# Batch 0's projection by seven block products, its value blocks copied by GpSimd in the setup

## The chip, the core and the metric

The kernel runs on one core of a Trainium2 chip. The core has five engines with a queue of instructions each: TensorE (PE; its weight loads are listed as PEld), VectorE (DVE), ScalarE (ACT), GpSimd (POOL) and SyncE (SP), which here only issues DMAs. An instruction starts when its predecessor on the same engine has been issued and the semaphores that it waits for are set. The metric is the device time of one execution in microseconds, the median of three runs.

## The reference

A graph attention layer over 16 batches of 512 nodes with 512 features. `cond` is one vector for each batch, `mask` an integer tensor of 512 x 512 x 11.

```python
self_feat = concat(x, where(x.sum(-1) == 0, 0, cond)) @ W_self.T + b_self   # (16, 512, 512)
output = self_feat
for d in range(2):                       # adjacency and its transpose
    A = adj[:, :, :20]                   # only the first 20 nodes are keys
    q = self_feat @ Wq[d].T + bq[d]      # 16 heads of 32
    k = self_feat[:, :20] @ Wk[d].T + bk[d]
    aff = where(A.sum(-1) > 0, q.k / sqrt(32), -9e15) + (A @ w_bias + b_bias)
    w = softmax(aff)                     # over 20 keys
    out = (w @ self_feat[:, :20]) through Wout[d], head by head, + bout[d]
    output += out
return x + relu(output)
```

## The kernel before

All data are float32 and features lie on the partitions (`P` = 128, `C` = 4 chunks of features). Queries are never formed: in the **setup** the keys are multiplied through `Wq` into a matrix for each batch (`g`, 128 x 4 x 608), and the values through `Wout` (`vw_d`, in HBM). A batch then needs `self_feat` (tile `sf`), the scores `sf` x `g`, a softmax, and a product with the values.

**Setup** (lines 458 to 764). After the first projections a loop of 22 *bursts* (`keys`, L674) makes the key matrices, three halves at a time: 12 matmuls into two PSUM tiles, which ScalarE (L689) and VectorE (L691) empty into staging tiles `st` (four buffers). From the staging tiles the key matrix goes to three places: for batch 0 into the SBUF tile `g0` (by SP DMAs for three of four feature chunks, by a GpSimd copy for the last), for batch 1 into `g1_d` and for the rest into `g_d`, both in HBM. All bursts use the same two PSUM tiles, so a burst starts when the previous one is emptied.

Between bursts TensorE does other work, which the string `plan` (L719) spreads over the bursts from the fifth on, one word for each burst: `v` and `w` are value steps (L649; a `w` is half of the rows), `c` score-bias steps (L622), `n` row flags (L189), `s` a quarter of one piece of batch 0's projection, `b` small biases on VectorE. GpSimd stores values and score biases in HBM by its own DMAs (L657, L636).

**Projection.** `self_feat` of the batches 1 to 15 is made by a scheme with seven block products in place of eight (`product`, L249): the weights and the columns of x after the first 20 are cut in 2 x 2 blocks, GpSimd forms sums of the x blocks (`x_sum`, L238, t1 to t4) and of the weight blocks (`weight_sums`, L223, once), TensorE does seven products of 16 matmuls of 246 columns (in the order 1, 2, 6, 7, 5, 4, 3), and VectorE puts the PSUM results together (`partial`, L289, which reads the bank that later products keep adding to, and `joined`, L299, which adds the other bank). A product that adds to a bank waits until the partial before it has read it. Batch 0 uses the plain projection instead (`self_feat`, L205, 128 matmuls of 236 or 256 columns): three quarters in the setup, the last at tile 1 of batch 0 in the loop. The first 20 columns are a copy of the setup's key features (`new_self`, L303).

**Loop** (lines 786 to 984). Each batch has four tiles (`nt`) of 128 nodes. A tile is: scores on TensorE (L365, two PSUM buffers of two banks), mask and bias added on VectorE (L379, with `full`, formed by GpSimd at L344), maximum and subtraction (L383, L387), exponential on ScalarE (L392), sum and reciprocal on VectorE (L415, L416), normalising on GpSimd (L417), transposing on VectorE (L424). The product with the values of batch b - 1 (`attend`, L435) stands at tile 2 of batch b, and the projection of batch b + 1 is spread over the tiles 2 and 3 of batch b and tile 0 of b + 1.

**Values.** `attend` wants the values in blocks with zeros between them. `clear_blocks` writes zeros over all of `bd_d` in HBM (2 MB), `blocks` copies the values of all batches from `vw_d` into it, HBM to HBM, in runs of 128 bytes by 12 DMAs, and `load_values` brings the blocks of one batch in.

**Queues.** The order on each queue is written out by hand. In the later batches a load on SP waits for a named instruction (`behind`), so that loads come one by one: for instance the first half of the next batch's mask after `done["masks"]`. In batch 0 SP instead issues, unthrottled: all keys of batch 1 ahead of the loop, at tile 1 the masks, score biases, the 2 MB of zeros and the row-sum inputs (`load_xn`), at tile 2 the 12 block copies, at tile 3 the values of batch 0. `row_sum` (L169, ScalarE) reads what `load_xn` brings; `mask_spread` (L337, ScalarE) copies the summed mask to the layout that `full` needs.

Of the kernel before, what the change touches and what calls it, by code (L numbers as in the profile page):

```python
# [13 lines left out]
P = 128  # L14
# [4 lines left out]
def gat_kernel(  # L19
# [64 lines left out]
    vw_d = dram.tile([2, C, BM, P], F32, name="vw_d")  # L84
    bd_d = dram.tile([C, B, 32, HL, 2, DH], F32, name="bd_d")
# [5 lines left out]
    adds, fulls, wts, outs, held, sf_ps, conds, prods = {}, {}, {}, [], [None] * 3, {}, {}, {}  # L91
    sums, parts, us, done = {}, {}, {}, {}
# [42 lines left out]
    def load_values(b, ins=None):  # L135

        vds[b] = gp.tile([P, HL, 2, DH], F32, tag="vd", name=f"vd{b}", bufs=1)
        for c in range(C):
            behind(nc.sync.dma_start(
                vds[b][bass.ts(c, 32)].rearrange("p e i g -> p (e i g)"), bd_d[c, b].rearrange("r e i g -> r (e i g)")  # L140
            ), ins if c == 0 else None)

    def clear_blocks(zero):

        nc.sync.dma_start(
            bd_d.rearrange("c b r e i g -> (c b r) (e i g)").rearrange("(n p) w -> p n w", p=P),
            zero.unsqueeze(1).to_broadcast([P, C * B * 32 // P, HL * 2 * DH]),
        )

    def blocks():  # L150

        bb = bd_d.rearrange("c b r e i g -> (c b) r e i g")
        vv = vw_d.rearrange("d c (b m) (e g) -> d (c b) m e g", m=NG, e=HL)
        for e in range(HL):
            for i in range(2):
                j = (e * S) // 32 + i
                for d in range(2):
                    lo = max(e * S + d * NG, 32 * j)
                    hi = min(e * S + (d + 1) * NG, 32 * j + 32)
                    if lo < hi:  # L160
                        m, r = lo - e * S - d * NG, lo - 32 * j
                        nc.sync.dma_start(bb[:, r : r + hi - lo, e, i], vv[d, :, m : m + hi - lo, e])


# [29 lines left out]
    def self_feat(b, f, h, parts=((0, range(C)), (1, range(C)))):  # L194


        lo, hi = max(NG, h * N // 2), (h + 1) * N // 2
        for i, ks in parts:
            if (i, ks[0]) == (0, 0):
                if (f, h) == (0, 0):  # L200
                    new_self(b)
                held[0] = bank(f"ps_sf{b}_{f}{h}", 3 if (f, h) == (1, 1) else None)
            for k in ks:
                for a in range(HL):
                    nc.tensor.matmul(  # L205
                        held[0][bass.ts(a, R), i * N // 2 : i * N // 2 + hi - lo],
                        ws_v[:, k, bass.ds((2 * f + i) * P + a * R, R)], xs[b][:, k, lo:hi],
                        start=(k == 0), stop=(k == C - 1),
                    )
            if (i, ks[-1]) == (1, C - 1):  # L210
                sf_ps[b, f, h] = held[0]

    def self_copy(b, f, h):

        lo, hi = max(NG, h * N // 2), (h + 1) * N // 2
        ps = sf_ps.pop((b, f, h))
        for i in range(2):
            nc.vector.scalar_tensor_tensor(
                sfs[b][:, 2 * f + i, lo:hi], nzs[b][:, lo:hi], qw[:, 2 * f + i, b : b + 1],
                ps[:, i * N // 2 : i * N // 2 + hi - lo], ALU.mult, ALU.add,  # L220
            )

# [15 lines left out]
    def x_sum(b, n):  # L238

        t = sums[b, n] = xsum.tile([P, 2, HN], F32, tag=f"t{n}", name=f"t{b}_{n}")  # L240
# [8 lines left out]
    def product(b, n):  # L249
# [11 lines left out]
        if n == 1:  # L261
            parts[b, "a"] = [bank(f"ps_a{b}_{i}", i) for i in range(2)]
        if n == 2:
            parts[b, "d"] = bank(f"ps_d{b}", 2)
        if n == 5:
            parts[b, "c"] = bank(f"ps_c{b}", 3)
# [30 lines left out]
    def joined(b, n, key, f, l):  # L297

        done["joined"] = nc.vector.tensor_add(  # L299
            block(b, f, l), parts[b, key][:, : 2 * HN].rearrange("p (i n) -> p i n", i=2), us.pop((b, n))  # L300
# [30 lines left out]
    def mask_spread(b, h, quarters=range(4)):  # L331

        add = conds[b, h]
        for a in quarters:
            for g in range(HL):
                r = bass.ts(g, R)
                nc.scalar.copy(adds[b, h][bass.ts(a, R), :, g], add[r].rearrange("p (t m) -> p t m", t=2))  # L337
# [38 lines left out]
    def weigh(b, nt, ps, between=None):  # L376

        f = softmax_view(fulls.pop((b, nt)))
        nc.vector.tensor_add(  # L379
# [78 lines left out]
    with tc.tile_pool(name="setup", bufs=1) as sp, tc.tile_pool(name="ps_acc", bufs=4, space=PSUM) as acc["pool"]:  # L458
# [157 lines left out]
        with tc.tile_pool(name="setup_g", bufs=4) as sg:  # L616

            def bias_scores(d):
# [7 lines left out]
                if d == 0:  # L626
                    stages["c"] = load.tile([P, 2, F], F32, tag="xn", name="c")
                    nc.gpsimd.memset(stages["c"][:, :, :BM], 0.0)
# [12 lines left out]
            def values(t, ds, k):  # L641
# [11 lines left out]
                if k == C - 1:  # L653
                    v = msk.tile([P, H * S], F32, tag="full", name=f"v{t}{ds[0]}")[:, :F]
                    nc.vector.tensor_copy(v, ps)
                    for i, d in enumerate(ds):
                        nc.gpsimd.dma_start(  # L657
                            vw_d[d, :, bass.ds(t * P, rows)].rearrange("c r w -> r c w"),
                            v[bass.ds(i * rows, rows)].rearrange("p (c w) -> p c w", c=C),
                        )  # L660

            stages = {}
            HB = B // 2

            def keys(runs):
# [14 lines left out]
                for fc, hg, d, lo, hi in runs:  # L680
# [12 lines left out]
                    if d == 1 and hi == 2:  # L693
                        to, of = g0[:, fc, bass.ts(hg, WD // C)], st[:, 0].rearrange("p h d m -> p (h d m)")
                        if fc < C - 1:
                            nc.sync.dma_start(to, of)
                        else:
                            nc.gpsimd.tensor_copy(to, of)
# [3 lines left out]
            def self_step(b, f, h, i, k):  # L702
                self_feat(b, f, h, ((i, (k,)),))
                if (i, k) == (1, C - 1):
                    self_copy(b, f, h)
# [6 lines left out]
                "s": [  # L712
                    (self_step, (0, f, h, i, k)) for f, h in ((0, 0), (1, 0), (0, 1))
# [353 lines left out]
```

## Time and profile before

| | |
|---|---|
| runs (us) | 585.79, 588.49, 589.13; median 588.49 |
| profiled execution (us) | 586.05 |
| its span, first to last instruction (us) | 583.9 |
| busiest engines | TensorE 575.7, VectorE 489.0, ScalarE 395.6, GpSimd 384.9 |
| HBM read, written | 82.30 MB, 40.24 MB |
| batch period from batch 1 on (us) | 30.5 |

How to read it: times are microseconds from the start of the span. TensorE executes a float32 matmul as two records, so 16 matmuls of a block product appear as x32. The four matmuls of a group work on different columns of the array at the same time, so the length of a piece in the chain, not the mean of one record, is what the piece costs. SPq and POOLq are the DMA-issuing sides of those queues; a DMA has an issue time on its queue and a time to landing.

### The profile page before, as it was taken

The numbers are of one execution on the slowest core, as the hardware profiler recorded it, in microseconds if no ns is written. First come the engines' busy times: TensorE is split into PE (matmuls) and PEld (weight loads), VectorE is DVE, ScalarE is ACT, GpSimd is POOL, SyncE is SP. The second block draws the span as 40 slices with busy tenths as digits, with TensorE's granted clock in tenths as the row PEclk, the third lists the DMA queues.
The fourth block names the chain that finished last, engine by engine and source line by source line (L and its number), as shares of the span: only waits on it lengthen the run. The fifth ranks groups of instructions, "written<-read, shape, count | busy, mean of one in ns | idle before, by whom it ended". The sixth has DMA issues, their size and how long they took to land.

```text
span 583.9 us, 30310 instructions
## 1 busy us (share of the span) xinstructions
PE 575.7 (99%) x13184; PEld 437.0 (75%) x13184; DVE 489.0 (84%) x783; ACT 395.6 (68%) x1162; POOL 384.9 (66%) x351
## 2 busy tenths in 40 slices
PE   9999999999999999999999999999999999999996
PEld 6654547887878787877878787787887878787873
DVE  0485565889898989899999999898989898989895
ACT  1334644586877777868686868687786877777671
POOL 2405663648778685858586777686868677776775
PEclk9999999999999999999999999999999999999999
DMA  8999899857766675757576767676676765664404
GB/s 303 388 407 311 331 377 320 273 123 213 209 197 196 185 214 169 217 167 217 168 214 171 214 171 212 177 199 188 199 202 187 199 198 172 199 199 114 144 15 146
DMA packets 103220, 124.14 MB, mean 213 GB/s; under 512 B 21712, under 2 KB 71920, under 8 KB 101040
## 3 DMA queue, kind: packets, MB, share of 16 engines
q1 hardware_dynamic: 101296, 119.79, 66.8%
q8 instruction: 104, 1.70, 1.3%
q0 software_dynamic: 672, 1.36, 1.0%
q10 hardware_dynamic: 1120, 1.06, 0.5%
q14 instruction: 28, 0.23, 0.2%
HBM read 82.30 MB, written 40.24 MB: 210 GB/s over the span
## 4 chain that ended last, share of the span: by engine, by line
PE 98%; DVE 0%; issue 0%; ACT 0%; DVEq 0%
PE ps_s L365 46%; PE ps_a L282 17%; PE ps_c L282 9%; PE ps_o L435 6%; PE ps_d L282 4%; PE ps_v L649 3%; PE ps_k L586 3%; PE ps_sf L205 2%; PE ps_kv L537 2%; PE ps_o L779 1%; PE ps_warm L496 1%; PE ps_nz L189 0%; PE ps_s L354 0%; PE ps_c L622 0%; PE ps_q L547 0%
## 5 line engine op out<-in xcount | busy, mean ns | idle before, releaser
L365 PEld LDWEIGHTS ps_s<-g,sf 128*32 128x32 f32 x8192 | 262.8, 110 | 20.9 <-issue 13.0
L365 PE MATMUL ps_s<-g,sf 128*32 128x152 f32 x8192 | 276.7, 293 | 0.5 <-ACT st L689 0.5
L337 ACT COPY both<-add 32x80 f32<-32x80 f32 x512 | 130.8, 256 | 53.8 <-DVE add L328 48.0
L417 POOL TENSOR_TENSOR s<-s,sm 128x640 f32<-128x640 f32 x63 | 80.4, 1276 | 94.2 <-DVE sm L416 68.2
L344 POOL TENSOR_TENSOR full<-cq,both 128x640 f32<-128x640 f32 x64 | 100.4, 1568 | 27.5 <-issue 21.3
L317 ACT ACTIVATE prod<-adj,wb_sb 128x80 f32<-128x80 int32 x330 | 112.4, 433 | 0.0
L392 ACT ACTIVATE s<-s 128x640 f32<-128x640 f32 x63 | 46.5, 738 | 64.1 <-DVE s L387 63.8
L449 POOL TENSOR_TENSOR o<-o,x 128x512 f32<-128x512 f32 x60 | 76.4, 1297 | 0.0
L379 DVE TENSOR_TENSOR full<-ps_s,full 128x608 f32<-128x608 f32 x63 | 48.8, 774 | 27.9 <-PE ps_s L365 22.6
L415 DVE TENSOR_REDUCE sm<-s 128x32 f32<-128x640 f32 x63 | 50.8, 806 | 9.5 <-ACT s L392 9.2
L282 PE MATMUL ps_a<-t,ws_s 128*32 128x246 f32 x960 | 55.4, 370 | 0.0
L383 DVE TENSOR_REDUCE ps_s<-full 128x32 f32<-128x640 f32 x63 | 52.2, 828 | 2.2
L424 DVE STREAM_TRANSPOSE wt<-s 128x640 f32<-128x640 f32 x63 | 52.7, 837 | 0.6 <-POOL s L417 0.6
L387 DVE TENSOR_TENSOR s<-full,ps_s 128x640 f32<-128x640 f32 x63 | 51.5, 817 | 1.1
L282 PEld LDWEIGHTS ps_a<-t,ws_s 128*32 128x32 f32 x960 | 31.6, 110 | 16.0
L328 DVE TENSOR_REDUCE add<-prod 128x80 f32<-128x960 f32 x32 | 36.8, 1150 | 6.2 <-ACT prod L317 4.4
L247 POOL TENSOR_TENSOR t<-x 128x492 f32<-128x492 f32 x30 | 34.6, 1153 | 9.5 <-DVE ps_s L383 5.4
L446 ACT ACTIVATE o<-o,bo 128x512 f32<-128x512 f32 x60 | 38.3, 713 | 0.6 <-DVE o L444 0.6
L435 PE MATMUL ps_o<-wt,vd 32*32 32x512 f32 (+5 forms) x816 | 36.7, 578 | 0.0
L444 DVE TENSOR_TENSOR o<-ps_o,sf 128x512 f32<-128x512 f32 x60 | 36.7, 668 | 0.0
L289 DVE SCALAR_TENSOR_TENSOR u<-nz,qw,ps_a 128x246 f32<-128x246 f32 x90 | 36.6, 448 | 0.0
L247 POOL TENSOR_TENSOR t<-x,t 128x492 f32<-128x492 f32 x30 | 34.5, 1150 | 2.3 <-DMA x<-in_xT 1.1
(239 smaller groups left out, 719.5 us busy)
## 6 DMA issues: line engine op xcount, KB each, us to landing
g_d<-st SPq DMA_DIRECT2D x16, 1064.0 KB, 5.9
g<-g_d SPq DMA_DIRECT2D x56, 304.0 KB, 3.6
out_T<-o SPq DMA_DIRECT2D x60, 256.0 KB, 3.3
x<-in_xT SPq DMA_DIRECT2D x56, 256.0 KB, 3.2
xn<-in_xn SPq DMA_DIRECT2D x52, 256.0 KB, 3.3
adj<-in_adj SPq DMA_DIRECT2D x56, 220.0 KB, 3.2
nz<-nz_d SPq DMA_DIRECT2D x14, 256.0 KB, 4.6
wk<-in_wkT SPq DMA_DIRECT2D x2, 1024.0 KB, 7.7
```

The lines of the kernel that those rows point to most:

```text
L247: done["xsum"] = nc.gpsimd.tensor_sub(t, one, two)
L282: nc.tensor.matmul(to, lhs, x[:, k], start=start, stop=stop, skip_group_check=n != 2)
L317: nc.scalar.activation(p[:, :, l], a[:, :, l], AF.Identity, scale=wb_sb[:, l : l + 1])
L337: nc.scalar.copy(adds[b, h][bass.ts(a, R), :, g], add[r].rearrange("p (t m) -> p t m", t=2))
L344: done["full"] = nc.gpsimd.tensor_add(f, cqs[b].unsqueeze(1).to_broadcast(shape), adds[b, nt // 2][:, nt % 2].unsqueeze(2).to_broadcast(sh ...
L365: nc.tensor.matmul(to, sfs[b][:, k, bass.ds(nt * P + (2 * g + j) * R, R)], of, start=(onto is None and k == 0 and (whole or j == 0)), stop ...
L383: nc.vector.tensor_reduce(mx, f, AX.X, ALU.max)
L387: done["weigh"] = nc.vector.tensor_sub(s, f, mx.unsqueeze(3).to_broadcast(full))
L417: done["normal"] = nc.gpsimd.tensor_mul(s, s, sm.unsqueeze(3).to_broadcast(full))
L424: nc.vector.transpose(wts[b][:, nt], s.rearrange("p a h m -> p (a h m)"))
L435: nc.tensor.matmul(banks[a][bass.ds(at // 2 * DH, n * DH)].rearrange("p (t n) -> p t n", n=32), vd[r, bass.ds(at * DH, n * DH)], wt[r, :, ...
L449: nc.gpsimd.tensor_add(o[:, c], o[:, c], xs[b][:, c])
```

## The change

Three things are changed together.

1. Batch 0's projection uses the seven block products, all in the setup: the plan has `p` in place of `s`, one product for each of the last seven bursts, followed at once by its `partial` or `joined`. The weight sums move to the fifth burst, batch 0's four x sums to burst 11 on GpSimd; their tile takes a buffer of `sf`. `partial` writes into `sf` itself in place of a tile of its own, for all batches, and so `new_self` stands at tile 2.
2. `bd_d` and `vw_d` are split at batch 5. Zeros and blocks of the first five batches are written in the setup by DMAs of GpSimd: `clear_first` at burst 7 (640 KB), 12 copies from burst 10 on (one for each burst). The other zeros are written by eight DMAs of SP in batches 1 to 3, the other 12 copies by SP in batches 4 and 5. All 16 pieces of `g0` are copied by GpSimd.
3. In batch 0 the loads for batch 1 (masks, score biases, keys) and the row-sum inputs of batch 2 each wait for a named instruction, as in later batches, and the values of batch 0 are loaded in batch 1.

```diff
-    vw_d = dram.tile([2, C, BM, P], F32, name="vw_d")
-    bd_d = dram.tile([C, B, 32, HL, 2, DH], F32, name="bd_d")
+    EARLY = 5
+    parts_of = ((0, EARLY), (EARLY, B))
+    vw_d = [dram.tile([2, C, (hi - lo) * NG, P], F32, name=f"vw_d{lo}") for lo, hi in parts_of]
+    bd_d = [dram.tile([C, hi - lo, 32, HL, 2, DH], F32, name=f"bd_d{lo}") for lo, hi in parts_of]
...
-    def clear_blocks(zero):
...
+    def clear_first():
+
+        n = C * EARLY * 32 // P
+        nc.gpsimd.dma_start(
+            bd_d[0].rearrange("c b r e i g -> (c b r) (e i g)").rearrange("(n p) w -> p n w", p=P),
+            zero.unsqueeze(1).to_broadcast([P, n, HL * 2 * DH]),
+        )
...
+    def clear_rest(n, ins):
+
+        rows = (B - EARLY) * 8
+        to = bd_d[1][n // 2].rearrange("b r e i g -> (b r) (e i g)").rearrange("(n p) w -> p n w", p=rows)
+        behind(nc.sync.dma_start(
+            to[:, n % 2 * 2 : n % 2 * 2 + 2], zero[:rows].unsqueeze(1).to_broadcast([rows, 2, HL * 2 * DH])
+        ), ins)
...
-                        nc.sync.dma_start(bb[:, r : r + hi - lo, e, i], vv[d, :, m : m + hi - lo, e])
+                        found.append((bb[:, r : r + hi - lo, e, i], vv[d, :, m : m + hi - lo, e]))
+        return found
+
+    def clears(b):
+
+        at = cleared.count(b)
+        cleared.append(b)
+        if b in (1, 2, 3) and (b, at) != (1, 0):
+            clear_rest(3 * b - 4 + at, done["exp" if at == 1 else "xsum"])
+
+    def spill(n, queue=nc.sync):
+
+        for _ in range(n):
+            queue.dma_start(*copies.pop(0))
...
-    def partial(b, n, f, l, to=None):
-
-        if to is None:
-            to = us[b, n] = xsum.tile([P, 2, HN], F32, tag=f"u{n}", name=f"u{b}_{n}")
+    def partial(b, f, l):
+
+        to = block(b, f, l)
...
-                        if fc < C - 1:
-                            nc.sync.dma_start(to, of)
-                        else:
-                            nc.gpsimd.tensor_copy(to, of)
+                        nc.gpsimd.tensor_copy(to, of)
...
+            def block_product(n):
+
+                product(0, n)
+                f, args = {
+                    1: (partial, (0, 0, 0)), 2: (joined, (0, "d", 0, 0)), 6: (partial, (0, 0, 1)),
+                    7: (partial, (0, 1, 1)), 5: (joined, (0, "c", 1, 1)), 4: (partial, (0, 1, 0)),
+                    3: (joined, (0, "c", 0, 1)),
+                }[n]
+                f(*args)
...
-            plan = "bvv vv vv ccw vv ns ssss sssw vv vv ssss ssss vv vv nww ssss ssss".split()
+            plan = "bvv vvc vvc vvn vv vvw vv vv w w wn p p p p p p p".split()
...
+                if n == 4:
+                    weight_sums()
+                if n == 7:
+                    clear_first()
+                if n == 9:
+                    row_sums(1)
+                    copies = blocks(0)
+                if n > 9:
+                    spill(1, nc.gpsimd)
                 if n == 11:
-                    row_sums(1)
-                if n == 13:
-                    weight_sums()
+                    new_self(0)
+                    for i in range(1, 5):
+                        x_sum(0, i)
...
-        load_keys(1)
-
...
-                if b == 0 and nt == 1:
-                    load_adj(1, 0)
-                    load_cq(1)
-                    clear_blocks(zero)
-                    load_adj(1, 1)
-                    load_xn(2, 0)
-                    load_xn(2, 1)
-                if b == 0 and nt == 2:
-                    blocks()
-                if nt == 2 and last or nt == 3 and b == 0:
+                if nt == 2 and last:
                     load_values(b)
...
                         if more:
                             load_adj(b + 1, 0, done["masks"], slice(0, 1))
+                        if b in (4, 5):
+                            copies = copies or blocks(1)
+                            spill(1)
                     mask_spread(b, 1, (0, 1))
+                    if b == 0:
+                        load_adj(1, 0, done["spread"], slice(0, 1))
...
-                    if b == 0:
-                        self_feat(0, 1, 1)
                     for g in range(2):
                         scores(b, nt, g, ps[g])
-                    if b == 0:
-                        self_copy(0, 1, 1)
...
-                    if b > 0 and more:
+                    if more:
                         load_keys(b + 1, range(1), done["normal"])
...
+                        new_self(b + 1)
-                    s = weigh(b, nt, pair, (lambda: partial(b + 1, 1, 0, 0)) if more else None)
+                    s = weigh(b, nt, pair, (lambda: partial(b + 1, 0, 0)) if more else None)
                     expo(s)
+                    if b == 0:
+                        load_xn(2, 1, done["exp"], slice(1, 2))
```

More of the change, by code (lines that the diff above doesn't have):

```diff
@@ L261, in product @@
         if n == 1:
-            parts[b, "a"] = [bank(f"ps_a{b}_{i}", i) for i in range(2)]
+            parts[b, "a"] = [bank(f"ps_a{b}_{i}", i if b else None) for i in range(2)]
         if n == 2:
-            parts[b, "d"] = bank(f"ps_d{b}", 2)
+            parts[b, "d"] = bank(f"ps_d{b}", 2 if b else None)
         if n == 5:
-            parts[b, "c"] = bank(f"ps_c{b}", 3)
+            parts[b, "c"] = bank(f"ps_c{b}", 3 if b else None)
         for i in range(2):
@@ L336, in mask_spread @@
                 r = bass.ts(g, R)
-                nc.scalar.copy(adds[b, h][bass.ts(a, R), :, g], add[r].rearrange("p (t m) -> p t m", t=2))
+                done["spread"] = nc.scalar.copy(adds[b, h][bass.ts(a, R), :, g], add[r].rearrange("p (t m) -> p t m", t=2))
     def full_add(b, nt):
@@ L656, in values @@
                     for i, d in enumerate(ds):
[L657 to L662, printed above, removed]
+                        edge = EARLY * NG
+                        for n, lo, hi in ((0, 0, edge), (1, edge, rows)) if t == 0 else ((1, 0, rows),):
+                            nc.gpsimd.dma_start(
+                                vw_d[n][d, :, bass.ds(t * P + lo - n * edge, hi - lo)].rearrange("c r w -> r c w"),
+                                v[bass.ds(i * rows + lo, hi - lo)].rearrange("p (c w) -> p c w", c=C),
+                            )
+            stages = {"c": load.tile([P, 2, F], F32, tag="xn", name="c")}
+            nc.gpsimd.memset(stages["c"][:, :, :BM], 0.0)
             HB = B // 2
@@ L922, in gat_kernel @@
                         full_add(b, NT - 1)
[L923 to L924 removed]
+                        load_keys(b + 1, range(1, 2), done["full"])
                     if b > 0:
```

125 lines of the change are left out of this document (53 added, 72 removed).

## The prediction

> **What bounds the kernel now.** I read the page first: the busy times by engine and the chain of work that ended last.
>
> ```profile
> span 583.9 us, 30310 instructions
> ...
> PE 575.7 (99%) x13184; PEld 437.0 (75%) x13184; DVE 489.0 (84%) x783; ACT 395.6 (68%) x1162; POOL 384.9 (66%) x351
> ...
> PE 98%; DVE 0%; issue 0%; ACT 0%; DVEq 0%
> ```
>
> TensorE has work in 99% of the span and carries 98% of the chain, so a microsecond of TensorE work or of TensorE waiting is a microsecond of the span; the 8.2 us left over is all that removed waiting could ever bring. To see whether that holds in the stages that change, I asked for the busy time of each engine by stretch (the columns are PE, PEld, DVE, ACT, POOL, clock, DMA share, GB/s):
>
> ```profile
> 39.00:91.40 52.40, 51.67 (x545) 24.90 (x544) 31.81 (x61) 24.48 (x57) 29.50 (x34) 1.00 0.95 346
> 91.40:120.60 29.20, 28.47 (x736) 24.60 (x740) 21.11 (x33) 16.63 (x55) 12.72 (x12) 1.00 0.90 267
> 120.60:151.10 30.50, 30.50 (x790) 24.68 (x784) 27.94 (x45) 23.25 (x69) 22.46 (x21) 1.00 0.68 191
> ```
>
> The second half of the setup (39.0 to 91.4) and batch 0 (91.4 to 120.6) wait 0.73 us each; batch 1 takes 30.50 us, all of it TensorE work, and later batches look the same. Their TensorE work is not changed, so the result is decided by when TensorE reaches batch 1, at 120.6 now, and by whether a new wait appears after it.
>
> **TensorE work.** The chain in order of time (start, length, what) shows the old projection (L205) and the block products (L282), among others:
>
> ```profile
> 40.55 1.91 PE ps_v L649 x4
> 43.44 1.91 PE ps_v L649 x4
> ...
> 73.27 1.73 PE ps_sf L205 x32
> ...
> 88.53 1.86 PE ps_sf L205 x32
> ...
> 95.72 3.45 PE ps_sf L205 x64
> 99.17 8.27 PE ps_s L365 x256
> 107.44 1.66 PE ps_a L282 x32
> ```
>
> Two value steps every 2.89 us with 1.91 us of their own leave 0.98 us for a burst of keys. The old projection costs four pieces at 1.73, two at 1.86 and 3.45 inside the loop: 14.1 us. In the setup a 256-wide piece costs 1.86, in the loop 3.45 / 2 = 1.73, so alternating with the bursts adds 0.14. A block product is 1.66 in the loop, so 1.80 in the setup, and seven cost 12.6. Net: 1.5 us less TensorE work, but 1.9 more in the setup and 3.45 less in batch 0.
>
> **The setup, slot by slot.** Each burst needs its two score banks emptied by VectorE and ScalarE before the next burst:
>
> ```profile
> 42.39 0.40 PE L674 MATMUL ps_g(0, 3, 1, 1, 2)0_409<-khD,wq_sb 32*128 32x152 f32 x2
> 49.17 1.23 PE L622 MATMUL ps_c<-khD,bqbd 128*32 128x304 f32 x16
> 50.33 1.08 PE L649 MATMUL ps_v<-wo_sb,kvT 128*64 128x512 f32 x4
> 55.22 1.12 PE L189 MATMUL ps_nz<-rx,ones 128*128 128x512 f32 x2
> 64.85 1.17 DVE L691 TENSOR_SCALAR st<-ps_g(2, 1, 0, 0, 2)1_636 128x608 f32<-128x608 f32 x2 [0.54 <-issue]
> 77.22 1.06 DVE L322 TENSOR_REDUCE cond<-adj 128x80 f32<-128x880 int32 x1
> 91.38 4.34 PE L365 MATMUL ps_s<-g,sf 128*32 128x152 f32 x128 [0.52 <-ACT st L689]
> 110.24 1.45 PE L282 MATMUL ps_d<-x,ws_v 128*32 128x246 f32 x24 [0.73 <-issue]
> 111.48 1.87 PE L282 MATMUL ps_a<-t,ws_s 128*32 128x246 f32 x32
> ```
>
> A slot can't be shorter than 0.98 + 1.17 and about 0.18 of signalling, 2.33 us. TensorE's order is the same up to the sixth burst, at 42.39. The rows give 0.95 for a value step, and, each less some 0.07 by which a last matmul's end overlaps the next start, 0.58 for one of two score-bias steps, 1.01 for a half-sized value step and 1.06 for row flags. The new plan is then two slots of 3.47, then 3.95, 2.89, 3.90, 2.89, 2.89, two of 2.33 (the lone "w" slots, whose own work is only 1.99, so 0.7 us of new waiting), 3.05, and seven of 0.98 + 1.80 = 2.78. I add 0.2 for the slot in which the mask count (1.06) delays VectorE's emptying beside a product. The sum is 50.8, so the first score matmul starts at 93.2 instead of 91.38. The 0.52 us wait there goes: the last product stands between the last burst and the scores.
>
> **Batch 0.** TensorE now has only scores there, and the softmax is late next:
>
> ```profile
> 95.84 0.79 DVE L379 TENSOR_TENSOR full<-ps_s,full 128x608 f32<-128x608 f32 x1 [3.07 <-issue]
> 103.43 0.79 DVE L379 TENSOR_TENSOR full<-ps_s,full 128x608 f32<-128x608 f32 x1 [2.25 <-POOL t L247]
> 107.87 0.73 DVE L379 TENSOR_TENSOR full<-ps_s,full 128x608 f32<-128x608 f32 x1
> 109.37 0.84 DVE L289 SCALAR_TENSOR_TENSOR u<-nz,qw,ps_a 128x246 f32<-128x246 f32 x2
> 100.63 1.27 POOL L417 TENSOR_TENSOR s<-s,sm 128x640 f32<-128x640 f32 x1 [2.02 <-DVE sm L416]
> 104.17 1.57 POOL L344 TENSOR_TENSOR full<-cq,both 128x640 f32<-128x640 f32 x1
> ```
>
> VectorE's first step follows the first score by 4.46 (91.38 to 95.84), so it starts at 97.66. GpSimd's normalising follows that by 4.79, at 102.45, and from there to the end of the third tile's bias it takes 100.63 to 105.74, 5.11 us: it ends at 107.55. VectorE, free for the second tile just before 102.45 (its scores end at 101.5), needs 103.43 to 107.87, 4.44, and would be ready at 106.8, so GpSimd decides. The partial block of batch 1 ends 2.34 after that start (107.87 to 110.21), at about 109.95. TensorE has done three score tiles (12.4) and two products (3.32) by 108.9 and waits 1.1 us; product 6 starts at 110.0 against 111.48. From there the program is the same, so the gain is **1.5 us**: the way from the first score to product 6 shrinks from 20.1 (111.48 - 91.38) to 16.8, and the setup grows by 1.8. The span comes to 582.4; the profiled execution took 586.05, so it becomes **584.6**.
>
> **What I cost at nothing, and its cover.** GpSimd gets most of the rest:
>
> ```profile
> 62.75 2.62 POOL L185 TENSOR_TENSOR rx<-rx,x 128x512 f32<-128x512 f32 x2
> 79.30 0.31 POOL L698 COPY g<-st 128x152 f32<-128x152 f32 x1
> 101.86 1.14 POOL L247 TENSOR_TENSOR t<-x,t 128x492 f32<-128x492 f32 x1
> L657 POOL DMA_DIRECT2D vw_d<-v x6: 622/818/987, 46.4 to 86.4; - x6
> L636 POOL DMA_DIRECT2D cq_d<-c x8: 620/622/697, 51.7 to 57.1; - x8
> L162 SPq DMA_DIRECT2D bd_d<-vw_d x12: 611/716/1692, 108.6 to 119.9; - x12
> bd_d<-zero SPq DMA_DIRECT2D x1, 2048.0 KB, 9.1
> vw_d<-v POOLq DMA_DIRECT2D x4, 256.0 KB, 4.4
> ```
>
> It had 29.5 us of work in the setup's second half. Added: four block sums (4.6), nine key copies (2.8), two more value stores (1.2), the clear and twelve copies. No row shows GpSimd copying from HBM to HBM in 128-byte runs. Its DMA instructions lie between 0.62 (64 runs) and 0.99 (512 runs); a copy has 80 to 400, so I take 0.8, 9.6 us in all. The bias add of tile 1 (1.6) falls behind the setup. That is about 47 of 54 us. In program order: the clear is issued near 59.9; its 640 KB lie between the 4.4 and the 9.1 us rows, say 5.5, while the row sums (three at 1.31) keep GpSimd until 65.9; the eleventh copy ends near 88.8. Its last key copy, on which the scores wait, can only start when the last burst is emptied near 92.7. So 3.9 us are spare over some 13 DMAs, and they cost nothing below **1.1 us** each; both rows lie under it. The weight sums move to a time when GpSimd had nothing.
>
> SP loses twelve key copies, the 2 MB clear and 12 block copies in a row. The clears return as eight of 176 KB in batches 1 to 3, the copies as six in each of batches 4 and 5, between loads that already wait for a signal. Six at 0.72 is 4.3 us of issue in 30.5. The load nearest to its user is the row-sum input:
>
> ```profile
> 239.21 4.26 ACT L337 COPY both<-add 32x80 f32<-32x80 f32 x16 [1.72 <-DVE add L328]
> 130.80 1.05 POOL L247 TENSOR_TENSOR t<-x 128x492 f32<-128x492 f32 x1 [4.10 <-DMA x<-in_xT]
> ```
>
> ScalarE, done with the row sums, idles 1.72 us for VectorE, and one copy ahead delays it by less than that. Batch 1's loads now come one by one; the last row is what the jam on SP costs today, a wait of 4.1 us off the chain, so the removal shows in no row of TensorE. The partial blocks written in place and the earlier copy of the first 20 columns are the same instructions.
>
> **Rivals.**
> (a) *GpSimd falls behind; slower.* Place: its last key copy. Above 1.1 us a DMA, every 0.1 us delays the first score by 1.3. At 1.69, the longest row of this transfer on SP, that is 12 x 0.6 = 7; with a clear that lands after 9.1, 3 more: 592 to 595. Against it: 14 GpSimd DMAs, none above 0.99. The Trainium skill (SBUF — State Buffer, section "SBUF: two separate sides") says that GpSimd can't write DMA descriptors while VectorE runs a two-port operation, and gives 620 ns alone against about 3100 beside a VectorE copy; worked out from its figures, an estimate, the sum would pass 600. The trace bears it out only in the unhindered figure: in this stretch VectorE reads PSUM.
> (b) *Batch 0's softmax takes back all.* If GpSimd enters the loop 1.5 us late, product 6 is as late as today: 586, up to the median of 588.5.
> (c) *Loads late in batches 1 to 5.* If an added copy costs more than the 1.72 us, four to five batches lose about 1 each: 589 to 590. Against it: the SP rows above.
> (d) *No wait at all.* Without the 1.1, 0.7 and 0.2: 582.6.
>
> **The numbers.** Forecast 0.55, (a) 0.20, (b) 0.10, (c) 0.10, (d) 0.05. The three runs before are 585.79, 588.49 and 589.13, so the profiled 586.05 lies at their lower end, 2.4 under the median; a part of that may be the jam on SP that goes, so I add 0.6 to the sum: **585.2 us**, 582.6 to 587.5 for this case alone. The range is 582 ((d), with scatter) to 595 (the end of (a)). About 0.5% is what a measurement of this kernel can tell from no change, 2.9 us: the forecast lies just across it, so its chance is split 0.36 to 0.19; (d) is faster; (b) is no change in 0.05 and slower in 0.05, since a late softmax seldom stops at zero; (a) and (c) are slower, but for 0.03 of (c) that ends within. That makes 0.41, 0.27 and 0.32.
>
> **What would show it.** First score matmul at 93.2 (within 0.7), product 6 of batch 1 at 110.0 with about 1 us of waiting before it that ends with VectorE's partial block; no wait of the first scores on GpSimd; GpSimd DMAs of 0.6 to 1.0; batches from 1 on at 30.5 with TensorE full. Wrong if GpSimd's copies exceed 1.1 us, if the evictions wait for GpSimd, or if a batch from 1 to 5 is longer than 30.5.

## The result, and the profile after

| | before | after |
|---|---|---|
| median of 22 runs, us | 587.66 (585.79 to 589.13) | 586.15 (584.42 to 587.70) |
| profiled execution, us | 586.05 | 584.8 |
| its span, us | 583.9 | 582.7 |

The ratio is 0.9974 with a 95% interval of 0.9963 to 0.9985: 1.5 us less (0.9 to 2.2), which is under the 0.5% that the prediction took as its bound for no change. The page of the changed kernel: span, busy times, the chain by engine.

```profile
span 582.7 us, 30297 instructions
...
PE 574.6 (99%) x13152; PEld 436.4 (75%) x13152; DVE 493.8 (85%) x786; ACT 395.5 (68%) x1162; POOL 403.8 (69%) x382
...
PE 94%; POOL 3%; issue 1%; DVE 1%; ACT 0%; DVEq 0%; POOLq 0%
```

TensorE has 1.1 us less work than before, GpSimd 18.9 us more, VectorE 4.8 more. The chain still is TensorE's. The chain in order of time (start, length, what) in the changed stretch:

```profile
80.34 1.80 PE ps_a L283 x32
...
93.32 12.40 PE ps_s L365 x384
105.72 1.66 PE ps_a L283 x32
107.38 1.66 PE ps_d L283 x32
109.04 0.62 issue
109.66 1.86 PE ps_a L283 x29
```

A block product takes 1.80 us in the setup; the first scores start at 93.32 without a wait, the three score tiles follow without the old projection between them, and product 6 of batch 1 waits 0.62 us and starts at 109.66 (before: 111.48). Busy time by stretch (us, PE, PEld, DVE, ACT, POOL, clock, DMA share, GB/s):

```profile
39.00:93.20 54.20, 53.86 (x576) 26.46 (x572) 36.20 (x63) 24.32 (x56) 46.78 (x61) 1.00 0.94 331
93.20:119.00 25.80, 25.18 (x680) 22.26 (x676) 20.83 (x32) 15.69 (x51) 11.87 (x10) 1.00 0.64 192
119.00:149.50 30.50, 30.50 (x787) 24.76 (x783) 27.83 (x45) 24.04 (x74) 22.47 (x21) 1.00 0.68 194
...
210.50:241.00 30.50, 29.85 (x773) 23.57 (x769) 27.19 (x44) 23.61 (x73) 22.08 (x19) 1.00 0.76 205
```

GpSimd now works 46.8 of the 54.2 us of the setup's second half. In batch 0 the DMA share falls from 0.90 to 0.64. Batch 4 (the last row) is not full: of the 1.8 us by which product 6 came earlier, 0.53 of them because the setup's first burst began sooner, 0.65 are lost again at 239.44, in the middle of a product. The rows of TensorE, VectorE and GpSimd (start, length, engine, line, what; in brackets the idle time before and what ended it):

```profile
41.48 2.79 DVE L610 TENSOR_SCALAR bqbd<-bqw 32x8 f32<-32x8 f32 x4
...
105.93 1.58 POOL L344 TENSOR_TENSOR full<-cq,both 128x640 f32<-128x640 f32 x1
...
107.54 0.79 DVE L379 TENSOR_TENSOR full<-ps_s,full 128x608 f32<-128x608 f32 x1 [0.93 <-POOL full L344]
109.10 0.84 DVE L289 SCALAR_TENSOR_TENSOR sf<-nz,qw,ps_a 128x246 f32<-128x246 f32 x2
...
239.44 0.83 PE L283 MATMUL ps_a<-t,ws_s 128*32 128x246 f32 x12 [0.65 <-issue]
```

VectorE's third tile waits for GpSimd's bias, as forecast (107.54 against 107.55). The four writes bqbd took 0.71 us before and 2.79 now; that was not forecast.

### The profile page after: what moved, and what is told of

Its sections match the earlier page's. It is cut to its first block, busy times and chain, and to the rows that moved or that the text cites. A ratio compares the mean times of both kernels' runs of the same rounds, so it can differ in the third digit from the quotient of the medians.

```text
span 582.7 us, 30297 instructions
## 1 busy us (share of the span) xinstructions
PE 574.6 (99%) x13152; PEld 436.4 (75%) x13152; DVE 493.8 (85%) x786; ACT 395.5 (68%) x1162; POOL 403.8 (69%) x382
## 4 chain that ended last, share of the span: by engine, by line
PE 94%; POOL 3%; issue 1%; DVE 1%; ACT 0%; DVEq 0%; POOLq 0%
PE ps_s L365 46%; PE ps_a L283 18%; PE ps_c L283 9%; PE ps_o L435 6%; PE ps_d L283 5%; PE ps_k L586 3%; PE ps_kv L537 2%; POOL cq_d L633 1%; PE ps_o L784 1%; PE ps_warm L496 1%; POOL vw_d L656 0%; DVE bqbd L610 0%; POOL prod L314 0%; PE ps_v L646 0%; DVE st L691 0%
## 5 line engine op out<-in xcount | busy, mean ns | idle before, releaser
L365 PEld LDWEIGHTS ps_s<-g,sf 128*32 128x32 f32 x8192 | 263.7, 110 | 20.1 <-issue 13.1
L283 PE MATMUL ps_a<-t,ws_s 128*32 128x246 f32 x1024 | 60.0, 371 | 1.3 <-issue 1.3
L415 DVE TENSOR_REDUCE sm<-s 128x32 f32<-128x640 f32 x63 | 50.8, 807 | 10.1 <-ACT s L392 9.9
L289 DVE SCALAR_TENSOR_TENSOR sf<-nz,qw,ps_a 128x246 f32<-128x246 f32 x128 | 51.6, 443 | 1.7 <-PE ps_a L283 1.7
L283 PEld LDWEIGHTS ps_a<-t,ws_s 128*32 128x32 f32 x1024 | 33.5, 110 | 19.6 <-issue 1.7
L248 POOL TENSOR_TENSOR t<-x 128x492 f32<-128x492 f32 x32 | 36.8, 1151 | 7.5 <-DMA g_d<-st 7.5
L248 POOL TENSOR_TENSOR t<-x,t 128x492 f32<-128x492 f32 x32 | 36.7, 1148 | 1.3
L193 ACT ACTIVATE xn<-xn 128x512 f32<-128x512 f32 x56 | 34.4, 616 | 3.6 <-DMA xn<-in_xn 3.6
```

The lines of the kernel that those rows point to most:

```text
L248: done["xsum"] = nc.gpsimd.tensor_sub(t, one, two)
L283: nc.tensor.matmul(to, lhs, x[:, k], start=start, stop=stop, skip_group_check=n != 2)
L289: done["partial"] = nc.vector.scalar_tensor_tensor(to[:, i], nzs[b][:, half(l)], qw[:, 2 * f + i, b : b + 1], parts[b, "a"][i][:, :HN], AL ...
L365: nc.tensor.matmul(to, sfs[b][:, k, bass.ds(nt * P + (2 * g + j) * R, R)], of, start=(onto is None and k == 0 and (whole or j == 0)), stop ...
```

## The experiments

The start of the setup's first burst of keys moves from execution to execution (24.74 to 26.81 in the 14 profiles), as the loads of the weights land; it comes before anything that is edited. So the table counts from it: in each profile the first score and the end of the span, less the start of that burst. Where the scores follow a product without a wait, their start is that product's end in the chain.

| kernel | first burst at | first score after it | end after it | ratio to before (95%) |
|---|---|---|---|---|
| before | 25.67 | 65.71 | 558.2 | 1 |
| after | 25.14 | 68.18 | 557.6 | 0.9974 (0.9963 to 0.9985) |
| 1 loads and copies alone | 25.76 | 68.64 | 561.1 | 1.0069 (1.0047 to 1.0090) |
| 2 products alone | 25.20 | 68.81 | 558.5 | 0.9993 (0.9979 to 1.0007) |
| 3 GpSimd's copies twice | 26.05 | 69.50 | 560.9 | 1.0015 (0.9996 to 1.0034) |
| 4 VectorE copies beside them | 25.95 | 75.23 | 563.5 | 1.0054 (1.0037 to 1.0070) |
| 5 after, weight sums apart | 24.74 | 68.42 | 558.7 | 0.9974 (0.9961 to 0.9988) |
| 6 as 2, sums apart | 26.02 | 67.52 | 557.2 | 0.9958 (0.9941 to 0.9974) |
| 7 as 1, sums apart, key copies on SP | 26.04 | 67.82 | 562.0 | 1.0035 (1.0017 to 1.0052) |
| 8 after, three edits | 26.31 | 67.04 | 557.1 | 0.9968 (0.9949 to 0.9986) |
| 9 as 1, sums apart, biases early | 25.85 | 66.79 | 560.6 | 0.9998 (0.9978 to 1.0019) |
| 10 as 6, two edits of 8 | 26.49 | 66.7 | 557.7 | 0.9960 (0.9944 to 0.9976) |
| 11 after again | 26.00 | 67.75 | 557.9 | 0.9976 (0.9959 to 0.9992) |
| 12 as 8, copies late | 26.81 | 67.35 | 556.6 | 0.9986 (0.9971 to 1.0000) |

The profiles of before and after differ by only 0.6 us at the end, before and 11 by 0.3; the 1.5 us rests on the medians.

### 1 and 2: the change taken apart

Experiment 1 keeps the new clears, copies and loads and puts back the old projection and its order of steps; experiment 2 is the kernel before with only the block products. Both write the partial blocks in place, as the changed kernel does. The edits here and below are shortened.

```
1:  -  plan = "bvv vvc vvc vvn vv vvw vv vv w w wn p p p p p p p"
    +  plan = "bvv vv vv ccw vv ns ssss sssw vv vv ssss ssss vv vv nww ssss ssss"
    +  if b == 0: self_feat(0, 1, 1)          (loop, second tile, then self_copy)
2:  the same plan line the other way round, on the kernel before, with
    +  if n == 4: weight_sums()               (was n == 13)
    +  if n == 11: new_self(0); x_sum(0, 1..4)
```

> The changed kernel with the old projection of batch 0 (24 pieces in the setup by the old order of steps, 3.45 us inside the loop); clears, copies and loads as in the changed kernel. Theory T (the gain is TensorE work: 14.1 us of old projection against 12.6 of block products): no gain, 586.0 to 588.5, within 0.2% of before; first score near 91.4 and 3.45 us of the old projection in batch 0. Rival R (the gain comes from taking the 2 MB clear and the row of copies off SP in batch 0): the whole gain, about 1.5 us, ratio 0.997, and product 6 of batch 1 about 1.5 earlier than 111.48.

> The kernel before with nothing but the seven block products in the setup: batch 0's loads, the 2 MB clear and the 24 copies stay on SP inside batch 0, and GpSimd gets only the four block sums. T: most of the gain, 1.0 to 1.9 us (ratio 0.9968 to 0.998); first score near 93.2, product 6 near 109.7; if TensorE's 0.7 us gap during the copies stays, 0.7 of it is lost after batch 0. R: no gain, ratio 1.000.

Neither came out as either theory said: 1 is 4 us slower, 2 gains next to nothing. The parts do not add up to the whole, so at least one of them alone met a cost that the whole avoids. The rows of 1 show two costs, both before the first score. In order of time, VectorE's writes bqbd and its mask sum:

```profile
42.08 2.79 DVE L639 TENSOR_SCALAR bqbd<-bqw 32x8 f32<-32x8 f32 x4
...
64.36 1.15 DVE L357 TENSOR_REDUCE add<-prod 128x80 f32<-128x960 f32 x1 [3.69 <-POOL prod L352]
```

GpSimd of the same execution beside bqbd:

```profile
41.89 1.28 POOL L253 TENSOR_TENSOR ws_s<-ws_v 128x512 f32<-128x512 f32 x1
43.14 1.27 POOL L254 TENSOR_TENSOR ws_s<-ws_v,ws_s 128x512 f32<-128x512 f32 x1
```

In the old order the score biases come late, so GpSimd, with the clear and a value store more, reaches the mask count late; VectorE stands before the mask sum for 3.69 us and empties no bank of the key bursts, and TensorE waits 1.51 us at 66.74. And bqbd, which reads and writes SBUF only, takes four times as long while GpSimd's sums run. In 2 GpSimd had no key copies ahead of the sums, ran them at 30.1 to 36.1, and met VectorE's bqt there. VectorE of experiment 2:

```profile
31.62 1.68 DVE L578 SCALAR_TENSOR_TENSOR bqt<-wq_sb,br_sb 128x512 f32<-128x512 f32 x1
```

TensorE of experiment 2, behind the emptying that came late for it:

```profile
36.66 0.40 PE L648 MATMUL ps_g(0, 2, 0, 1, 2)1_358<-khD,wq_sb 32*128 32x152 f32 x2 [0.93 <-DVE st L665]
```

bqt takes 0.68 us where GpSimd is idle. The Trainium skill (SBUF — State Buffer, section "SBUF: two separate sides") has this as a rule: VectorE and GpSimd share one pair of SBUF ports, which one instruction holds to its end, and a VectorE instruction with two SBUF inputs is held up only by a GpSimd one that reads SBUF. The row of bqt, which has two SBUF inputs, agrees: 1.68 against 0.68. bqbd reads one tensor only, so that sentence does not cover it; its 2.79 against 0.71 shows that it is held up too, and no run shows in which mode it works.

### 3 and 4: GpSimd's cover, and the rule on its DMAs

```
3:  queue.dma_start(to, of)
    + if queue is nc.gpsimd: queue.dma_start(spare, of)
4:  spill(1, nc.gpsimd)
    + for _ in range(2): nc.vector.tensor_copy(scratch, br_sb)
```

> The changed kernel with each of GpSimd's 12 copies issued a second time, into a spare buffer that nobody reads. By the spare of 3.9 us (the prediction's): 12 x 0.72 = 8.6 us more on GpSimd, 11 of the 12 before its last key copy, so the last key copy comes 7.9 later less about 3.0 of idle time that is there now (1.54 + 0.39 + 1.04), and the first score, on which it stands 2.6 before, moves by about 2.3: 1.5 to 4 us slower than the changed kernel. If GpSimd were far from the path, nothing would change (within 0.5 us).

> The changed kernel with two VectorE copies of 512 elements from SBUF to SBUF (result not used) in each of the 12 slots in which GpSimd issues a copy. By the rows so far (0.64 to 0.78 us for a GpSimd DMA beside VectorE's work on PSUM): GpSimd's DMAs keep 0.6 to 0.9, VectorE gets about 24 x 0.3 = 7 us more in slots where it has some 0.9 free each, and the time rises by 0 to 3 us. By the Trainium skill (SBUF: State Buffer, section SBUF: two separate sides) a GpSimd DMA that meets such a copy takes about 3.1 us: several of the 12 then are above 1.1 and the first score comes 5 us or more late.

Experiment 3: 8.1 us of added copies make the kernel 0.41% slower than the changed one, 2.4 us. The scores begin, and after 30 records wait for GpSimd's last key copy; TensorE had lost 1.16 us without a releaser before, in a product, and but for that the wait would have been longer:

```profile
92.25 1.03 PE L287 MATMUL ps_a<-t,ws_v 128*32 128x246 f32 x14 [1.16 <-issue]
...
97.03 1.24 PE L369 MATMUL ps_s<-g,sf 128*32 128x152 f32 x32 [0.46 <-POOL g L699]
```

So the cover is real and finite: about 5 us of GpSimd work fit in (7.4 before the last key copy, less the 2.4 by which the median is longer; an estimate, since not all of the 2.4 need be this wait), near the 3.9 of the prediction. Experiment 4, GpSimd's group of copies (busy us in all, mean ns of one; then idle time before them):

```profile
L187 POOL DMA_DIRECT2D bd_d<-vw_d x12 | 8.5, 711 | 1.8 <-DVE scratch L763 1.3 <-issue 0.5
```

VectorE's group of added copies in the same stretch:

```profile
L763 DVE COPY scratch<-br_sb 128x512 f32<-128x512 f32 x24 | 20.2, 841 | 0.4
```

Two pairs of them in order of time:

```profile
80.34 3.22 DVE L763 COPY scratch<-br_sb 128x512 f32<-128x512 f32 x2
...
89.44 0.88 DVE L763 COPY scratch<-br_sb 128x512 f32<-128x512 f32 x2
```

GpSimd beside the first pair:

```profile
81.15 2.11 POOL L314 TENSOR_TENSOR prod<-prod,wb_sb 128x880 f32<-128x880 f32 x1
```

GpSimd's copies stay at 0.71 us; one of the twelve starts 1.26 late behind a VectorE copy. The Trainium skill's 3.1 us for such a DMA is in no row. What gives way is VectorE: a pair of copies takes 0.88 alone and 3.22 while GpSimd's product of masks runs, 20.2 us for 24 where 10.6 would do. The first score comes 7 us later, and the time is 4.7 us longer (1.0054 against 0.9974), above the 0 to 3 that were expected: VectorE empties the banks later (TensorE waits 1.68 us for it at 84.79). Rival (a) had the right pair of engines, and the wrong victim.

### 5, 6, 7 and 9: the two costs taken out

```
  -  if n == 4: weight_sums()
  +  if 0 < n < 5: weight_sum(n - 1)        each behind done["kh"], VectorE's scaled keys
7 also:  key copies of fc < 3 back on SP
9 also:  plan = "bvv vvc vc vw vv ns ssss ..."
```

> The changed kernel with its four weight sums on GpSimd issued one by one, each behind a VectorE step on PSUM (the scaled keys), so that none runs beside VectorE's four writes bqbd from SBUF to SBUF. Those took 2.79 us in the changed kernel and in the first experiment, where GpSimd's weight sums ran at that time, and 0.71 in the kernel before and in the second, where GpSimd was idle. Theory S (VectorE's SBUF-to-SBUF work and GpSimd's take turns): bqbd at 0.71 again, the slot of 3.93 us at 45.50 shrinks to 3.47, first score 0.4 to 0.5 us earlier (92.9), the time 0.2 to 0.7 us less. If not S, bqbd stays at 2.79.

> The second experiment (block products only, on the kernel before) with the weight sums placed as in the fifth. There they ran at 30.1 to 36.1 beside VectorE's products bqt (1.68 to 1.75 us instead of 0.68) and TensorE waited 0.93 us at 36.66. S together with T (TensorE work): no wait there, first score near 93.1 instead of 94.0, and the ratio to the kernel before 0.9965 to 0.9985. If T is wrong, 0.9993 as before.

> The first experiment (clears, copies and loads only, old projection) with the weight sums placed as in the fifth and 12 of the 16 key copies back on SP. Its first score came 3.0 us late: 1.0 in the slot at 45.45 (bqbd at 2.79), 1.8 in the slot at 64.45, where VectorE's emptying waited until GpSimd had freed a staging tile. If these are its causes: first score at 91.4 to 92.2, the ratio 0.999 to 1.002 instead of 1.0069. If the copies and loads cost time by themselves (DMA traffic), 1.004 or more.

> Clears, copies and loads of the changed kernel, all 16 key copies on GpSimd, the old projection, the weight sums as in the fifth experiment, and the two score biases taken up two slots earlier (bvv vvc vc vw vv ns ..., the rest of the old order unchanged). In the first and the seventh experiment VectorE's mask sum stood 3.4 us in wait for GpSimd's mask count, which came behind the clear and one more value store, and TensorE lost 1.5 to 1.8 us there. If that is the cause: no such wait, first score 65.5 to 66.3 after the first burst of keys (65.7 in the kernel before, 68.6 and 67.8 in those two) and a ratio of 0.999 to 1.002. If the copies and the loads cost time by themselves, 1.003 or more again.

Experiment 5: bqbd is back at 0.72, and its slot shrinks by 0.39 (3.54 against 3.93); but the sums now meet bqt (up to 1.74 us), so two earlier slots grow by 0.35 and 0.70, and the time is unchanged. The theory S holds, the edit was no gain. VectorE's bqbd in experiment 5:

```profile
42.04 0.72 DVE L609 TENSOR_SCALAR bqbd<-bqw 32x8 f32<-32x8 f32 x4
```

TensorE there, which now waits in the slot before (0.21 us in the changed kernel):

```profile
40.13 0.40 PE L673 MATMUL ps_g(0, 3, 0, 0, 2)0_392<-khD,wq_sb 32*128 32x152 f32 x2 [0.92 <-DVE khD L592]
```

Experiment 6, the products alone without the long collision: 0.9958, 2.5 us less than before (1.5 to 3.5), a little under the expected range. With the weight sums so placed, the block products carry the whole gain, and perhaps more than the changed kernel shows. Experiment 7 missed: with the key copies on SP the wait for the mask count stayed (3.40), so staging tiles that GpSimd frees late, the cause that its expectation named, were not it. VectorE's mask sum in 7:

```profile
63.82 1.15 DVE L356 TENSOR_REDUCE add<-prod 128x80 f32<-128x960 f32 x1 [3.40 <-POOL prod L351]
```

The same in 9:

```profile
62.20 1.15 DVE L356 TENSOR_REDUCE add<-prod 128x80 f32<-128x960 f32 x1 [1.01 <-POOL prod L351]
```

With the biases two slots earlier the wait falls to 1.01, TensorE no longer waits there, and the ratio is 0.9998. Its first score still comes 1.08 later than before, 0.5 more than expected: two slots are longer by 0.48 and 0.70, as the sums beside bqt made them in 5. So clears, copies and loads show neither cost nor gain (0.9978 to 1.0019, about 1.3 us either way), if GpSimd reaches the mask count in time, and it is the new order of steps that sees to that.

### 8, 10, 11 and 12: a better version, and the loop

```
8:  sums apart;  plan = "bvv vvc vvc vv vn vv vv vv vw ww wn p p p p p p p"
    batch 0, second tile:  full_add(0, 2) ahead of x_sum(1, 2)
10: experiment 6 with this plan and this full_add
11: the changed kernel
12: experiment 8; of the six copies of batches 4 and 5 the last three
    behind load_x(b + 2, range(1, 2)) in the fourth tile
```

> The changed kernel with three edits: the weight sums as in the fifth; an order of steps without lone value steps (bvv vvc vvc vv vn vv vv vv vw ww wn, then the seven products); and in batch 0 GpSimd's bias of the third tile ahead of the second block sum. First score: 93.3 less 0.46 (weight sums), less 0.34 x 2 (lone slots), less 0.4 (the slot with row flags, 3.45 against 3.05) = 91.8; the 0.62 us wait before product 6 goes, so product 6 at 109.66 - 1.5 - 0.6 = 107.5. Time 1 to 2.2 us under the changed kernel, ratio to the kernel before 0.9935 to 0.996. If TensorE's order is not what decides, no gain.

> The sixth experiment (block products alone, sums apart; clears, copies and loads as in the kernel before) with the order of steps and the early bias of the third tile from the eighth. If the block products carry the whole gain and the waits are as read: TensorE reaches product 6 about 1.1 (lone slots) plus up to 0.6 (bias) sooner than in the sixth, ratio to the kernel before 0.993 to 0.9955. If the clears and copies on SP in batch 0 hold it back, no better than the sixth (0.9958).

> The changed kernel once more, on the same chip as the ninth and tenth: ratio 0.996 to 0.9985 again. Its first burst of keys began at 25.14 in the first profile and between 24.74 and 26.31 in all the profiles so far; if that start and TensorE's single stalls of 0.3 to 1.1 us inside a run of matmuls vary from execution to execution, the stall in batch 4 (0.65 us at 239.44) is not there again, or is elsewhere, and the span differs by up to 1.5 us from 582.7.

> The eighth experiment with three of the six value-block copies on SP of each of batches 4 and 5 moved from among the row-sum loads (xn) to behind the loads of x in the fourth tile, so that no copy but three early ones stands ahead of the last xn loads. In the profiles so far with copies in these batches ScalarE waited for xn there (1.0 to 3.7 us in a batch), its idle time before the mask spread shrank from 1.88 to between 0 and 1.6, and in five of seven kernels TensorE once lost 0.3 to 1.2 us in batch 4 or 5; without copies in the batch it was 1.88 each time. If the copies delay xn: the idle time before the spread is 1.5 to 1.88 in both batches, TensorE loses nothing there, and the time is 0 to 1 us under the eighth (ratio to the kernel before 0.9945 to 0.9975). If the loads are late for another reason, ScalarE waits for xn as before.

Experiment 8 reaches the first score 0.7 to 1.1 us sooner than the changed kernel (67.04 against 67.75 and 68.18) instead of 1.5: the slots from 43 to 73 us give 1.17, and the sums beside bqt lengthen an earlier one by 0.44. Product 6 no longer waits. But in its profile ScalarE waits in batch 0 for the row-sum input, and TensorE then for a partial block:

```profile
112.92 0.63 ACT L193 ACTIVATE xn<-xn 128x512 f32<-128x512 f32 x1 [2.12 <-DMA xn<-in_xn]
...
123.71 2.40 PE L364 MATMUL ps_s<-g,sf 128*32 128x152 f32 x64 [1.21 <-DVE sf L288]
```

That is as much as the earlier first score brought; no value-block copy stands on SP in batch 0, so the loads that wait for named instructions can come late there by themselves. The ratio, 0.9968, misses the expected range and can't be told from the changed kernel's. Experiment 10 has the first score 0.8 sooner than 6 and loses it again in a stall of 1.55 us inside the scores; no better than 6. Both products-only versions beat the kernel before; against the changed kernel (0.9974 and 0.9976) their 0.9958 and 0.9960 are lower, with intervals that overlap.

Experiment 11 repeats the time. The stall at 239.44 is not there again; another of 0.81 us stands inside the first scores, and 0.32 is lost in batch 5. Losses of this second kind, in batches 4 and 5, have a cause that can be read. ScalarE in batch 4 of experiment 9:

```profile
241.18 0.63 ACT L193 ACTIVATE xn<-xn 128x512 f32<-128x512 f32 x1 [2.05 <-DMA xn<-in_xn]
241.71 0.19 ACT L193 ACTIVATION_READ_ACCUMULATOR xn<-xn 128x1 f32 x1
241.81 4.24 ACT L365 COPY both<-add 32x80 f32<-32x80 f32 x16
```

VectorE behind it:

```profile
246.84 0.82 DVE L443 TENSOR_REDUCE sm<-s 128x32 f32<-128x640 f32 x1 [2.71 <-ACT s L420]
```

And TensorE:

```profile
248.39 0.85 PE L393 MATMUL ps_s<-g,sf 128*32 128x152 f32 x16 [1.17 <-DVE sf L317]
```

The row-sum input, with copies on SP among its loads, lands late, ScalarE's spread of the masks starts late, the exponentials behind it too, VectorE's sums wait for them, and TensorE for the partial block: 1.17 us. Without copies in the loop (experiments 2, 6, 10) ScalarE's idle time before the spread is 1.88 in batches 4 and 5. ScalarE of the changed kernel in these two batches:

```profile
237.25 4.27 ACT L337 COPY both<-add 32x80 f32<-32x80 f32 x16 [0.78 <-DVE add L328]
...
268.76 1.33 ACT L337 COPY both<-add 32x80 f32<-32x80 f32 x5 [0.35 <-DVE add L328]
```

ScalarE of 12, in which the last three copies stand behind these loads:

```profile
238.64 4.27 ACT L336 COPY both<-add 32x80 f32<-32x80 f32 x16 [1.88 <-DVE add L327]
...
269.20 2.93 ACT L336 COPY both<-add 32x80 f32<-32x80 f32 x11 [1.04 <-DVE add L327]
```

In 12 no wait for xn is left in these batches (the idle time is 1.88 in batch 4, but 1.04 and not the expected 1.5 in batch 5), TensorE shows no wait after product 6, and from the first burst on its profile is the shortest of all, 556.6. The median over its runs, 586.19, is not: 0.9986 misses the expected range. The profile of one execution and the median of twelve differ by such amounts here, and no version was shown to beat the changed kernel.

## Why the prediction was right

**The sum.** Forecast: 1.5 us less, from TensorE work; measured: 1.5 (0.9 to 2.2). The products are 1.80 us each in the setup as forecast, and experiments 6 and 10 show that they alone, with the weight sums apart, bring 2.4 to 2.5 us. That the two 1.5 agree is partly luck: terms of both signs were missed, as the next paragraphs say. And against the 588.49 of the three runs the 585.2 was 3.3 us less, just across the 0.5% bound; measured is half of that, on the other side of the bound, the outcome that had the chance of 0.27. The level, 585.2, was 0.95 too low because the profiled execution before (586.05) lay 1.6 under what turned out to be the median, and I had allowed 0.6.

**The setup.** First score at 93.2 forecast, 93.32 found; but it began 0.44 sooner, so the slots took 51.4 instead of 50.8. The difference is made up of misses of both signs; the larger ones, read from the starts of the bursts: 0.46 for bqbd, 0.40 for the slot with row flags (the lone steps' waiting ran on into it, as it seems), 0.34 for one product of 2.15 (it stands where the last section finds stalls), against 0.20 less in the third slot, 0.16 less in the lone slots and 0.44 less in the last one, whose burst is short. The step that failed is "the weight sums move to a time when GpSimd had nothing": that looked at GpSimd alone. VectorE's work of that time was the price.

**Batch 0.** GpSimd decides over VectorE, as forecast, to 0.01 us. The wait before product 6 is 0.62 instead of 1.1: product 6 starts behind the first half of the partial block (109.56), not behind its end (109.94).

**Cover and prices.** GpSimd's copies were 0.64 to 0.78 and its clear 0.94, against 0.8, its total 46.8 against 47; with that rival (a) fell. Its last key copy starts at 90.37 and does not wait for the last burst, near 92.7, as the forecast had it; that the spare comes near 3.9 all the same is in part luck.

**The loads, rival (c).** "One copy ahead delays it by less than that" failed. Not one copy's issue but the landing of the loads behind several is late, and the slack of 1.88 is used up: of the nine profiles of kernels with the copies so placed, four (experiments 3, 7, 9, 11) have a wait of TensorE of 0.3 to 1.2 us behind this in batch 4 or 5, and four (1, 4, 5, 8) have none; the stall of the changed kernel's own profile is of another kind (last section). (The expectation of 12 had counted seven kernels.) The place was right, the price per batch too high, and batch 0 can be hit as well (experiment 8).

**The jam on SP.** The sum gave its removal nothing, and the times show no gain from it: experiment 9 (without the jam) has 0.9998, experiment 6 (with it) 0.9958. That a part of the 2.4 us between profile and median was the jam, as the level had it, is not borne out either. But "shows in no row of TensorE" was wrong for batch 0. The way of 20.1 us from the first score to product 6 held a wait of 0.73 (110.24 in the lines of the prediction), which the forecast let go without a reason. With the old loads TensorE stands at this place of its instruction stream in all four kernels (before, 2, 6, 10: 0.68 to 1.02 us), with the new loads in none of ten, whichever projection they have. TensorE of experiment 6:

```profile
111.56 1.65 PE L258 MATMUL ps_a<-t,ws_s 128*32 128x246 f32 x26 [0.94 <-issue]
```

In the changed kernel a wait of 0.62 for the partial block stands there instead, so little is gained there; in experiments 8 and 12 neither stands. What in the old loads brings the wait was not tried.

## What to carry to other kernels

An edit that moves work to an idle engine has to be priced on the engines beside it too: for work moved to GpSimd, ask what VectorE does from SBUF to SBUF at that time. When a change of several parts is taken apart, a part can be slower alone than the whole, because another part (here the order of steps) pays its price; look for that wait before the part is called costly. Where single executions differ by more than the effect, count from the last event before the edit, and don't rank versions by one profile.

## What the hardware showed that was not expected

The start of the keys' first burst lies anywhere from 24.74 to 26.81 us; that is as much as the whole effect. In eight of the fourteen profiles a wait for the load of the weights `ws_q` shows ahead of it, 1.92 us in experiment 12. And TensorE stalls in single places inside a run of matmuls, with no releaser in the trace. TensorE of experiment 11, in the first score tile:

```profile
96.88 1.37 PE L365 MATMUL ps_s<-g,sf 128*32 128x152 f32 x36 [0.81 <-issue]
```

TensorE of experiment 12, in the second:

```profile
101.99 1.24 PE L364 MATMUL ps_s<-g,sf 128*32 128x152 f32 x32 [1.37 <-issue]
```

Nine of the fourteen profiles have one of 0.3 to 1.6 us within batch 0's scores, in eight of them after some 72, 200 or 327 of the 384 matmuls. The trace tells more than these rows. Queue q8 of the page brings instructions, in packets of 16 KB:

```profile
q8 instruction: 103, 1.69, 1.2%
```

In the changed kernel these 103 packets serve 26,523 records of TensorE, matmuls and weight loads together, some 256 to a packet. The stalls lie 128 matmuls apart, which with their weight loads is 256 records. All 15 stalls of over 0.25 us without a releaser from the first burst on, in batch 0's scores and elsewhere (the one in batch 4 and those of the old loads too; the wait for the partial block before product 6, read above, is not counted), stand at the same place of such a group of 256, and end 1.3 to 1.6 us after a q8 packet has landed; and of the 1432 groups of all profiles none begins less than 1.25 us after its packet. So TensorE waits there for its own instructions. Why a packet comes late was not tried and stays open.
